# LU blocks of a mixture-of-experts stage on one core: base copied from PSUM tile to PSUM tile, ranks accumulated there, output products issued one by one

## The chip, the cores and the metric

The kernel runs on one core of one Trainium2 chip. The metric is the device time of that core in microseconds (us), as the median of several executions. One execution was also profiled; all lines below are from it. Line numbers such as L1092 are lines of the kernel before the change.

The core has five engines that run their own instruction queues in order and wait for each other by semaphores. TensorE (PE in the profile, PEld for its weight loads) multiplies matrices and writes only to PSUM. VectorE (DVE) and ScalarE (ACT) do elementwise work and read and write both SBUF and PSUM. GpSimd (POOL) does elementwise work in SBUF here and issues the gathers and scatters by index. SyncE (SP) issues the other transfers. In this kernel PSUM is cut into banks of 128 x 512 fp32 numbers. A tile of shape [128, 2, 512] takes two banks.

## The reference, cut to what matters

The input has 4 x 1024 tokens of 256 numbers. A linear-attention layer with a feed-forward part comes first, then a layer of 8 experts that share the matrices w1, w3, w2 and differ by low ranks of 16 (a1, b1, a3, b3, a2, b2):

```
x = x + layernorm(attention_and_ffn(layernorm(x)))        # 4096 tokens of 256
t = rmsnorm(layernorm(x))
probs = softmax(t @ gate_w.T); topw, topi = top_k(probs, 2); topw /= sum(topw)
base1, base3 = t @ w1.T, t @ w3.T                          # 1024 wide, shared by all experts
for each expert e:
    h1[e] = base1 + 2 * (t @ a1[e].T) @ b1[e].T
    h3[e] = base3 + 2 * (t @ a3[e].T) @ b3[e].T
    act[e] = silu(h1[e]) * h3[e]
    out[e] = act[e] @ w2.T + 2 * (act[e] @ a2[e].T) @ b2[e].T
x = x + layernorm(sum over the two chosen experts of weight[e] * out[e])
```

## The kernel before, in words

**Attention part.** The tokens are worked in 8 blocks of 512 (`BLK`). Each block passes through `front` (normalize, queries, keys), `middle` (attention, feed-forward) and, in two halves, `tail` (gate, choice of the two experts, scatter of the token rows into an array `rows` in DRAM, sorted by class).

**Expert part.** The sorted rows are taken back in 8 blocks of 512 tokens, in the order of the list `ORDER`: block 0, 1, 2 of kind LU, 3 H, 4 G, 5 H, 6 G, 7 LU. In an LU block each token has one expert among the first four and one among the last four. In the H and G blocks the two experts lie otherwise. `prepare` (L870) loads the rows of a block and builds the transposed tokens `tT`, the masks `m0` and `m1`, the weights `wt` and the ranks `u0`.

**An LU block** is worked by `experts` (L1008) in eight steps f = 0 to 7, one for each 128 of the 1024 hidden features:

1. `base(f)` (L1019) multiplies `tT` by the slices of w1 and w3 into a two-bank PSUM tile `ph`: four products of 512 columns. The tile comes from a pool with two buffers, so that step f+1 can write one while step f is read from the other.
2. `copied` (L1102) lets ScalarE copy both banks of `ph` to an SBUF tile `copy` (L1105).
3. `halved` (L1080) adds the ranks. For the expert of the lower half TensorE adds them onto `ph`. For the upper one it writes the ranks alone to a second two-bank tile `py`, and VectorE adds the copy to it (L1092, 1024 columns). Products of the lower and the upper half use 64 rows of the array each and run side by side. Then ScalarE takes tanh of the first bank of each tile (L1090, L1094), and VectorE makes the two activations in four operations (L1097, L1098).
4. `mixed` (L1071) defers three GpSimd operations (L1078) that weight the two activations into a slice of `actA` (f below 4) or `actB`.
5. `down_lu` (L1109) multiplies the activations of step f-2 by a2 into a bank `pya`, and VectorE adds that to `yacc` (L1116).

After the eight steps the stream `finishing` (L1236) takes a buffer of the pool of `ph` for the output `po` and multiplies the slices of `actA`/`actB` by w2: 32 products of 256 columns (`up`, L1163), issued in batches, and four with b2. `finish` (L1167) has ScalarE copy one half of `po` after the other to `tT` (L1177). `end` (L1183) normalizes, and GpSimd adds the residual and scatters the rows to the output (L1225, L856). The main loop of the next block starts only when all `finishing` streams are done (L1125); its first `base(0)` comes ahead of that.

**The order of the work** is written by a planner in the kernel itself when it is built. Every piece of work is a Python generator (`Stream`) that yields a time at which it may go on. `now()` counts planned TensorE time; `V`, `A` and `G` count planned time of VectorE, ScalarE and GpSimd. At each point the planner takes the first stream that may run: a side stream (`sides`, L1335: ends, preparations, tails, fronts, middles, and last `finals`, the outputs), or else the main loop of the present block. The result is one fixed order for each engine. GpSimd work is put in a list (`defer`, L218) and issued by `catch_up` (L221). While the expert blocks run, the side streams share two one-bank PSUM tiles (`ps`).

The eight PSUM banks: two one-bank tiles `ps`, two two-bank buffers for `ph` and `po`, one two-bank tile `py`.

Of the kernel before, what the change touches and what calls it, by code (L numbers as in the profile page):

```python
# [8 lines left out]
F32 = mybir.dt.float32  # L9
# [42 lines left out]
def sandwich_kernel(  # L52
# [37 lines left out]
    phh = ctx.enter_context(tc.tile_pool(name="phh", bufs=2, space=PSUM))  # L90
# [104 lines left out]
    homes = [(ps, "ps"), (ps, "ps"), (phh, "ph"), (phh, "ph"), (pyy, "py")]  # L195
# [20 lines left out]
    later = []  # L216
# [4 lines left out]
    def catch_up(key=None, soon=None):  # L221

        while later:
            if soon is not None and max(free["G"], later[0][1]) > soon:
                break
            if key is not None and key not in [k for k, *_ in later]:
                break
            _, after, cost, do = later.pop(0)
            do()
            G(cost, after)  # L230
# [60 lines left out]
    def rsqrt(mv, eps, name, after=0.0):  # L291

        n = mv.shape[1]
        a = small([P, n], "rsa", f"rsa_{name}", 8)
        r = small([P, n], "rs", f"rs_{name}", 8)
        nc.vector.tensor_scalar(a, mv[:, :, 1], eps, None, ALU.add)  # L296
        nc.gpsimd.tensor_tensor(r, a, neghalf[:, 0:n], ALU.pow)  # L297
        return a, r, G(1.1, V(0.25, after))

    def rsqrt2(mv, eps, eps2, name, tag, after=0.0):  # L300


        n = mv.shape[1]
        a = small([P, 2, n], "r2a", f"r2a_{name}", 6)
        q = small([P, n], "r2q", f"r2q_{name}", 6)
        r = small([P, 2, n], tag, f"r2_{name}", 6)
        nc.vector.tensor_scalar(a[:, 0, :], mv[:, :, 1], eps, None, ALU.add)
        nc.vector.reciprocal(q, a[:, 0, :])
        nc.vector.tensor_tensor(q, q, mv[:, :, 1], ALU.mult)
        nc.vector.tensor_scalar(a[:, 1, :], q, eps2, None, ALU.add)  # L310
        nc.gpsimd.tensor_tensor(  # L311
            r.rearrange("p a t -> p (a t)"), a.rearrange("p a t -> p (a t)"),
            neghalf[:, 0 : 2 * n], ALU.pow,
        )
        return r, G(1.1 if n < TB else 1.65, V(1.1, after))
# [402 lines left out]
    def tail(i, hf, y, mv, e):  # L718
# [105 lines left out]
        e = V(3.2)  # L824
        for j in range(HT):
            scatter(rows, to[:, j : j + 1], xt[:, o + j, :], ROWS - 1, "rows")
# [41 lines left out]
    moe, taken, ended = {}, set(), set()  # L868
# [139 lines left out]
    def experts(n, kind):  # L1008
# [10 lines left out]
        def base(f):  # L1019
            ph = phh.tile([P, 2, BLK], F32, tag="ph", name=f"ph_{n}_{f}")  # L1020
            fs = slice(f * P, (f + 1) * P)
            for a, (w, _) in enumerate(W13):
                for c in range(DC):
                    if kind == "H":

                        for h in range(2):
                            mm(ph[:, h, a * HB : (a + 1) * HB], w[:, c, fs],
                               tT[:, c, h * HB : (h + 1) * HB], a == 0 and c == 0, False,
                               skip_group_check=True)
                    else:  # L1030
                        mm(ph[:, a, :], w[:, c, fs], tT[:, c, :], c == 0,
                           kind == "LU" and c == DC - 1)
            return ph
# [37 lines left out]
        def mixed(f, acts, e):  # L1071

            ac = halves[f // 4][:, f % 4, :]
            for k, (x0, x1, op) in enumerate((
                (acts[1], acts[0], ALU.subtract), (ac, wt, ALU.mult), (ac, acts[0], ALU.add)
            )):
                defer((n, f, k), e, 1.28,
                      lambda x0=x0, x1=x1, op=op: nc.gpsimd.tensor_tensor(ac, x0, x1, op))  # L1078

        def halved(f, ph, bc):  # L1080


            fs = slice(f * P, (f + 1) * P)
            for a, (_, bw) in enumerate(W13):
                mm(ph[:, a, :], bw[low, fs], us[0][low, a, :], False, True, skip_group_check=True)
                mm(py[:, a, :], bw[high, fs], us[0][high, a, :], True, True)
            at = now() + 0.2
            catch_up((n, f - 2, 2))
            acts = [new(f"act{k}", f"act{k}_{f}") for k in range(2)]
            nc.scalar.activation(acts[0], ph[:, 0, :], AF.Tanh, scale=0.5)  # L1090
            e0 = A(0.6, at)
            nc.vector.tensor_tensor(py, py, bc, ALU.add)  # L1092
            e1 = V(1.22, at)
            nc.scalar.activation(acts[1], py[:, 0, :], AF.Tanh, scale=0.5)  # L1094
            e1 = A(0.6, e1)
            for h, act, e in ((ph, acts[0], e0), (py, acts[1], e1)):
                nc.vector.scalar_tensor_tensor(act, act, 1.0, h[:, 0, :], ALU.add, ALU.mult)  # L1097
                nc.vector.tensor_tensor(act, act, h[:, 1, :], ALU.mult)  # L1098
                e = V(1.38, e)
            return acts, e  # L1100

        def copied(f, ph):  # L1102
            bc = mp1.tile([P, 2, BLK], F32, tag="copy", name=f"copy_{n}_{f}")
            for a in range(2):
                nc.scalar.copy(bc[:, a, :], ph[:, a, :])  # L1105
                e = A(0.6, now() + 0.2 - 1.7 * (1 - a))
            return bc, e
# [11 lines left out]
        ph = base(0)  # L1119
        if kind == "LU":  # L1120
            bc, e = copied(0, ph)
        else:
            e = 0.0
        yield max(ready, e)
        yield lambda: all(f.done for f in finals)  # L1125

        py = pyy.tile([P, 2, BLK], F32, tag="py", name=f"py_{n}")
        halves = [mp1.tile([P, FC // 2, BLK], F32, tag=t, name=f"{t}_{n}") for t in ("actA", "actB")]
        pend = []
        if kind == "LU":  # L1130
            yacc = mp1.tile([P, BLK], F32, tag="yacc", name=f"yacc_{n}")
            for f in range(FC):
                if f:
                    ph = base(f)
                    bc, e = copied(f, ph)
                    yield max(e, ea - 1.0)
                if f > 1:
                    down_lu(f - 2, pend.pop(0))
                acts, ea = halved(f, ph, bc)
                mixed(f, acts, ea)  # L1140
                pend.append(acts)
                yield 0.0
            e = ea
        else:
            for f in range(FC):
                a0, e = inner(f, 0, ph)
                nxt = base(f + 1) if f < FC - 1 else None
                yield e
                a1, e = inner(f, 1, ph)
                if f:  # L1150
                    down(f - 1, pend.pop())
                pend.append((a0, a1))
                ph = nxt
                mixed(f, pend[0], e)
                yield 0.0

        o = tT.rearrange("p c n -> p (c n)").rearrange("p (t d) -> p t d", d=D)
        po = None
# [8 lines left out]
        def finish(jj, ym):  # L1167
# [15 lines left out]
        def end(jj, m):  # L1183
# [11 lines left out]
            nc.vector.tensor_scalar(a[:, 0:m], mv[:, 0:m, 1], 1e-5, None, ALU.add)  # L1195
            nc.gpsimd.tensor_tensor(r[:, 0:m], a[:, 0:m], neghalf[:, 0:m], ALU.pow)
            yield G(1.0, V(0.15))
# [36 lines left out]
        ea = e  # L1234

        def finishing():  # L1236
            nonlocal po
            po = phh.tile([P, 2, BLK], F32, tag="ph", name=f"po_{n}")
# [8 lines left out]
            if kind == "LU":  # L1247
                for f in (FC - 2, FC - 1):
                    e = down_lu(f, pend.pop(0))
                nc.vector.tensor_tensor(ym, yacc, m1, ALU.mult)  # L1250
                e = V(0.69)
            else:
                down(FC - 1, pend[0])
                y1 = new("act1", "ym1")
                if kind == "H":
                    m, w, w0 = HB, m1[:, 0:HB], m0[:, 0:HB]
                    w1_, p0, p1 = m0[:, HB:BLK], py[:, 0, 0:HB], py[:, 0, HB:BLK]
                else:
                    m, w, w0, w1_, p0, p1 = BLK, wt, m0, m1, py[:, 0, :], py[:, 1, :]
                y0, y1 = ym[:, 0:m], y1[:, 0:m]  # L1260
                nc.vector.tensor_tensor(y0, p0, w0, ALU.mult)
                nc.vector.tensor_tensor(y1, p1, w1_, ALU.mult)
                nc.vector.tensor_tensor(y1, y1, y0, ALU.subtract)
                nc.vector.tensor_tensor(y1, y1, w, ALU.mult)
                nc.vector.tensor_tensor(y0, y0, y1, ALU.add)
                e = V(3.5 * m / BLK, now() + 0.2)
# [6 lines left out]
            finish(0, ym)  # L1273
            final = n == len(ORDER) - 1
# [4 lines left out]
            finish(2, ym)  # L1279
            closing.append(Stream(always, lambda: end(2, 2) if final else end(0, TB)))  # L1280

        finals.append(Stream(always, finishing))
# [6 lines left out]
    class Stream:  # L1289
# [5 lines left out]
        def can(self):  # L1295
            if self.done or not self.may() or min(slots) > now() + 0.2:
                return False
# [16 lines left out]
    with tc.manual_schedule(engines={EN.PE, EN.DVE, EN.Activation, EN.Pool}):  # L1314
# [20 lines left out]
        def sides():  # L1335
# [7 lines left out]
            yield from finals  # L1343
# [4 lines left out]

        def wait(main=None):

            at = [s.ready for s in [*sides(), *([main] if main else [])] if not s.done]
# [4 lines left out]
        for n, (kind, _, after, _) in enumerate(ORDER):  # L1356
            while not ready[n].done:
                s = side()
# [6 lines left out]
            while not main.done:  # L1365
# [3 lines left out]
                elif main.may() and main.ready <= now():  # L1369
                    main.may = always  # L1370
                    main.step()
                else:
                    wait(main)
        while not all(f.done for f in finals):
            s = side()
# [14 lines left out]
    with tc.If(lacking > 0):  # L1390
        with tc.For_i(0, NBLK, 1) as i:
# [6 lines left out]
            for _ in experts("all", "G"):  # L1398
                pass
            for streams in (finals, closing):  # L1400
# [51 lines left out]
```

## Time and profile before

| | |
|---|---|
| median of 3 runs | 1235.14 us (1229.81 to 1235.17) |
| the profiled execution | 1235.22 us, of which 1233.3 us from the first to the last instruction |
| mean granted TensorE clock | 0.966 of full speed |
| LU blocks 0, 1, 2, from the first product into `ph` to the last | about 255 to 345, 480 to 575, 640 to 735 us |
| H, G, H, G (blocks 3 to 6) | about 735 to 1145 us |
| LU block 7 and the end | 1145 to 1233 us |
| VectorE, add of the copy (L1092) | 32 times 1229 ns |
| ScalarE, copies (L1105) | 64 times 589 ns |
| GpSimd, mixing (L1078) | 192 times 1268 to 1340 ns |

The table's times per instruction are means of the groups by line. A span of an engine in the timeline is written as start, duration, engine, line, operation and tiles; the bracket at its end gives how long the engine was idle before and what ended that. One fp32 product is executed as two passes, so four products of `base` show as x8.

### The profile page before, as it was taken

The page shows a single profiled execution, that of the slowest core. Times are in us where ns is not written, and L with a number is a line of the kernel's source. Part 1 is how long each engine was busy: PE and PEld are TensorE (multiplying, and loading weights), DVE is VectorE, ACT ScalarE, POOL GpSimd, SP SyncE. Part 2 cuts the span into 40 slices and gives each one's busy share as a digit, 9 for nine tenths or more (in the row PEclk, how much of TensorE's full clock was granted, in tenths as well). Part 3 has the DMA queues.
Part 4 walks back from the last instruction along what each step waited for, and adds up shares of the span by engine and source line. Part 5 has one row for each costly group of instructions (what it writes and reads, how often), then busy time and mean ns, then how long its engine had stood idle before and what let it go on. Part 6 is the DMA issues. An engine that isn't in the chain of part 4 may idle for free. (4 is left out here: it accounts for less than half of the span.)

```text
span 1233.3 us, 13129 instructions
## 1 busy us (share of the span) xinstructions
PE 1116.3 (91%) x4700; PEld 753.3 (61%) x4700; DVE 657.9 (53%) x1908; ACT 363.4 (29%) x696; POOL 400.4 (32%) x394
## 2 busy tenths in 40 slices
PE   6879997998998899998999889989999999999894
PEld 5658886864477676574764457756544776445333
DVE  3583676658675547657438636435342353342462
ACT  1535443423433423322233222212111121221330
POOL 2010121123431103443214433175173183452552
PEclk9999998999998999998999898999999999999998
DMA  9800001100000100100100100010010010000000
GB/s 329 182 17 18 27 23 57 53 18 27 27 1 18 53 2 17 43 10 18 53 1 26 36 8 14 14 44 1 0 35 1 1 35 1 14 22 1 18 0 19
DMA packets 25590, 39.45 MB, mean 32 GB/s; under 512 B 2352, under 2 KB 19120, under 8 KB 25520
## 3 DMA queue, kind: packets, MB, share of 16 engines
q1 hardware_dynamic: 21344, 28.88, 7.7%
q0 software_dynamic: 3072, 8.49, 1.9%
q10 hardware_dynamic: 1104, 1.19, 0.3%
q8 instruction: 39, 0.64, 0.2%
q14 instruction: 31, 0.25, 0.1%
HBM read 21.48 MB, written 17.07 MB: 31 GB/s over the span
## 5 line engine op out<-in xcount | busy, mean ns | idle before, releaser
L261 PE MATMUL ph<-tT,w_s 128*128 128x512 f32 (+1 forms) x640 | 236.3, 517 | 6.9 <-DVE act L1040 4.4
L261 PEld LDWEIGHTS ph<-tT,w_s 128*128 128x128 f32 x640 | 120.2, 193 | 106.7 <-issue 93.6
L261 PE MATMUL ph<-u,b_s 64*128 64x256 f32 (+2 forms) x512 | 165.7, 518 | 17.1 <-DVE act L1040 8.9
L261 PEld LDWEIGHTS ph<-u,b_s 64*128 64x128 f32 (+1 forms) x512 | 69.2, 192 | 99.0 <-issue 62.8
L261 PE MATMUL pf<-h2T,wff_s 128*128 128x256 f32 x512 | 117.9, 385 | 6.5 <-DVE u L981 4.1
L1039 DVE SCALAR_TENSOR_TENSOR act<-act,ph 128x512 f32<-128x512 f32 x64 | 44.0, 688 | 147.6 <-ACT act L1037 147.6
L261 PE MATMUL py<-wff2d,g 128*128 128x256 f32 x512 | 115.7, 379 | 0.0
L261 PEld LDWEIGHTS pf<-h2T,wff_s 128*128 128x128 f32 x512 | 96.7, 191 | 24.8 <-issue 8.6
L261 PEld LDWEIGHTS py<-wff2d,g 128*128 128x128 f32 x512 | 97.4, 190 | 13.1
L1037 ACT ACTIVATE act<-ph 128x512 f32<-128x512 f32 x64 | 38.2, 597 | 162.5 <-PE ph L261 143.7
L856 POOL DMA_INDIRECT rows<-x,to x32 | 33.0, 1030 | 158.5 <-DVE to L823 53.8
L311 POOL TENSOR_TENSOR r_x<-r2a_x,neghalf 128x4 f32<-128x4 f32 (+1 forms) x24 | 30.8, 1285 | 150.7 <-DVE r2a_x L310 124.7
L675 ACT ACTIVATE g<-pf,bff 128x256 f32<-128x256 f32 x128 | 53.1, 471 | 87.1 <-PE pf L261 87.0
L1078 POOL TENSOR_TENSOR actB<-act,act 128x512 f32<-128x512 f32 x32 | 41.7, 1304 | 102.4 <-DVE act L1040 61.3
L261 PE MATMUL po<-w_s,actA 128*128 128x256 f32 x256 | 65.1, 399 | 6.5 <-ACT tT L1177 6.5
L297 POOL TENSOR_TENSOR rs_y<-rsa_y,neghalf 128x2 f32<-128x2 f32 x16 | 12.8, 798 | 176.3 <-DVE rsa_y L296 153.5
L261 PE MATMUL po<-w_s,actB 128*128 128x256 f32 x256 | 63.5, 387 | 5.7 <-POOL actB L1078 5.7
L261 PE MATMUL py<-u,b_s 64*128 64x512 f32 x128 | 67.1, 647 | 0.0
L261 PEld LDWEIGHTS po<-w_s,actA 128*128 128x128 f32 x256 | 49.2, 198 | 23.3 <-ACT tT L1177 9.7
L701 DVE SCALAR_TENSOR_TENSOR x<-py,std,x 128x256 f32<-128x256 f32 x32 | 15.4, 483 | 89.2 <-PE py L261 89.2
L1092 DVE TENSOR_TENSOR py<-py,copy 128x1024 f32<-128x1024 f32 x32 | 39.3, 1229 | 37.0 <-PE py L261 37.0
L261 PEld LDWEIGHTS po<-w_s,actB 128*128 128x128 f32 x256 | 49.4, 194 | 14.7 <-POOL actB L1078 6.7
(256 smaller groups left out, 1900.4 us busy)
## 6 DMA issues: line engine op xcount, KB each, us to landing
rows<-none SPq DMA_DIRECT2D x1, 4192.0 KB, 24.1
kept<-x SPq DMA_DIRECT2D x16, 262.0 KB, 2.1
row<-rows SPq DMA_DIRECT2D x8, 524.0 KB, 4.2
z<-in_x_dram SPq DMA_DIRECT2D x8, 512.0 KB, 3.4
x<-in_x_dram SPq DMA_DIRECT2D x8, 512.0 KB, 4.7
w_s<-in_w_dram SPq DMA_DIRECT2D x3, 1024.0 KB, 12.3
wff_s<-in_wff_dram SPq DMA_DIRECT2D x2, 1024.0 KB, 10.7
b_s<-in_b_dram SPq DMA_DIRECT2D x2, 512.0 KB, 11.5
```

The lines of the kernel that those rows point to most:

```text
L261: nc.tensor.matmul(out_, lhsT=lhsT, rhs=rhs, start=start, stop=stop, **kw)
L297: nc.gpsimd.tensor_tensor(r, a, neghalf[:, 0:n], ALU.pow)
L311: nc.gpsimd.tensor_tensor(r.rearrange("p a t -> p (a t)"), a.rearrange("p a t -> p (a t)"), neghalf[:, 0 : 2 * n], ALU.pow,)
L675: nc.scalar.activation(g[:, k * W : (k + 1) * W], pf[:, k * W : (k + 1) * W], AF.Gelu_apprx_tanh, bias=bff1_s[:, f : f + 1],)
L701: nc.vector.scalar_tensor_tensor(y[:, j, :], py[:, D : 2 * D], std[:, j : j + 1], y[:, j, :], ALU.mult, ALU.add)
L856: ins = nc.gpsimd.indirect_dma_start(out=dst[:, :], out_offset=bass.IndirectOffsetOnAxis(ap=at, axis=0), in_=src, in_offset=None, bounds_c ...
L1037: nc.scalar.activation(th, h1, AF.Tanh, scale=0.5)
L1039: nc.vector.scalar_tensor_tensor(th, th, 1.0, h1, ALU.add, ALU.mult)
L1078: lambda x0=x0, x1=x1, op=op: nc.gpsimd.tensor_tensor(ac, x0, x1, op))
L1092: nc.vector.tensor_tensor(py, py, bc, ALU.add)
```

## The change

It does five things.

- **The base goes from `ph` to `py` by ScalarE, and TensorE adds both ranks.** `base(f, ph, a)` now makes one half (a = 0: w1, a = 1: w3). After each half ScalarE copies that bank of `ph` to the same bank of `py`. The upper ranks are accumulated onto `py` as the lower ones onto `ph`. The VectorE addition (L1092) and the SBUF copy go away. In step 0 of block 0 the base of `py` is instead computed a second time by TensorE.
- **Two single buffers in place of a pool of two.** The tags `ph0` and `ph1` have one buffer each. An LU block uses one of them (`mine`) for all of its `ph`, and the other is for the output `po`.
- **Output products as a stream.** `output` yields after every single product, and the planner takes it (`filler`) only when neither a side stream nor the main loop can run. An LU block starts once the block before it has released `py` (`left`), with that block's outputs still to come.
- **GpSimd's list** is issued ahead of a power operation or a scatter where it is planned to be through by then (`catch_up(by=e)`).
- **Last block, step 7:** the three mixing operations run on VectorE. `down_lu` takes step f-1 in place of f-2.

```
-    phh = ctx.enter_context(tc.tile_pool(name="phh", bufs=2, space=PSUM))
+    phh = ctx.enter_context(tc.tile_pool(name="phh", bufs=1, space=PSUM))
...
-    def catch_up(key=None, soon=None):
+    def catch_up(key=None, soon=None, by=None):
...
+            if by is not None and max(free["G"], now(), later[0][1]) + later[0][2] > by + 0.3:
+                break
...
-        def halved(f, ph, bc):
+        def halved(f, ph):
             fs = slice(f * P, (f + 1) * P)
             for a, (_, bw) in enumerate(W13):
-                mm(ph[:, a, :], bw[low, fs], us[0][low, a, :], False, True, skip_group_check=True)
-                mm(py[:, a, :], bw[high, fs], us[0][high, a, :], True, True)
+                for bank, r in ((ph, low), (py, high)):
+                    mm(bank[:, a, :], bw[r, fs], us[0][r, a, :], False, True, skip_group_check=True)
...
-            nc.vector.tensor_tensor(py, py, bc, ALU.add)
...
+            for f in range(FC):
+                if f % 4 == 0:
+                    yield lambda: n == 0 or upped.get(n - 1, 0) >= f + 4
+                    value_tiles(f // 4)
+                yield e
+                ph = banks(mine, f"ph_{n}_{f}")
+                for a in range(2):
+                    base(f, ph, a)
+                    if n + f:
+                        nc.scalar.copy(py[:, a, :], ph[:, a, :])
+                        e = A(0.6, max(e1, now() + 0.2))
+                    else:
+                        base(f, py, a)
+                yield e - 0.4
+                if f:
+                    down_lu(f - 1, pend)
+                pend, (e, e1) = halved(f, ph)
+                mixed(f, pend, e1)
+                yield 0.0
...
+        def output(ahead):
+            nonlocal po
+            yield lambda: ahead is None or ahead.done
+            po = banks(1 - mine, f"po_{n}")
+            for f in range(FC):
+                yield lambda: (n, f, 2) in at_end
+                yield at_end[n, f, 2]
+                for j in range(TB):
+                    up(j, f)
+                    if j == TB - 1:
+                        upped[n] = f + 1
+                    yield 0.0
...
+                elif main.can(False):
                     main.step()
+                elif filler():
+                    filler().step()
```

H and G blocks keep their loops and their batched output (now named `rest`). They take the buffers of `ph` in turn (`whole_base`, `pair`), and the first `base` of a G block now stands ahead of the output products of the H block before it.

## The prediction

> **What bounds the kernel now.** I read the busy shares first, then TensorE's waits, then the timeline of the last LU block, where nothing but the block itself runs.
>
> ```profile
> span 1233.3 us, 13129 instructions
> PE 1116.3 (91%) x4700; PEld 753.3 (61%) x4700; DVE 657.9 (53%) x1908; ACT 363.4 (29%) x696; POOL 400.4 (32%) x394
> ```
>
> TensorE is busy for 91%, and the change takes no product away. It can only remove TensorE's idle time (117 us) or add to it. So I count the waits of TensorE, before and after.
>
> ```profile
> PE ph L261 <- ACT copy L1105: 8.2, 11, 2.6
> ...
> PE po L261 <- POOL actB L1078: 5.7, 2, 3.0
> ```
>
> (Total us, times, longest us.) The wait for the copy that the change works on is small: 8.2 us. Now one step of the last block:
>
> ```profile
> 1170.13 0.69 PE L261 MATMUL ph<-u,b_s 64*128 64x512 f32 x1 [0.21 <-ACT copy L1105]
> ...
> 1172.05 3.70 PE L261 MATMUL ph<-tT,w_s 128*128 128x512 f32 x8
> 1172.21 0.60 ACT L1090 ACTIVATE act<-ph 128x512 f32<-128x512 f32 x1 [2.13 <-PE py L261]
> 1172.26 1.23 DVE L1092 TENSOR_TENSOR py<-py,copy 128x1024 f32<-128x1024 f32 x1 [1.60 <-PE py L261]
> ...
> 1175.44 0.69 DVE L1098 TENSOR_TENSOR act<-act,py 128x512 f32<-128x512 f32 x1
> ...
> 1175.68 1.08 PE L261 MATMUL pya<-act,a_s 128*64 128x512 f32 x4
> 1175.84 1.07 ACT L1105 COPY copy<-ph 128x512 f32<-128x512 f32 x2 [1.72 <-PE ph L261]
> ...
> 1176.97 0.69 PE L261 MATMUL ph<-u,b_s 64*128 64x512 f32 x1 [0.21 <-ACT copy L1105]
> ```
>
> The next base (1172.05) runs while ScalarE and VectorE still work on this step, until 1176.13: two buffers allow it. The beat is 1176.97 - 1170.13 = 6.84 us, nearly all of it products. The third thing to see is what TensorE does between two banks of one tile:
>
> ```profile
> 1211.92 1.03 PE L261 MATMUL po<-b_s,ym 128*128 128x256 f32 x4
> 1212.99 0.60 ACT L1177 ACTIVATE tT<-po 128x512 f32<-128x512 f32 x1 [11.52 <-PE po L261]
> ...
> 1213.64 1.99 PE L261 MATMUL po<-w_s,actA 128*128 128x256 f32 x8 [0.69 <-ACT tT L1177]
> ```
>
> ScalarE reads the first bank of `po`, and TensorE, whose next products go to the second bank, waits for it to end. Issue of the four passes ends at 1211.92 + 4 x 0.213 = 1212.77 (a 512-column pass takes 0.427, by the eight passes from 1172.05 on), so this costs 0.87 us.
>
> **The change, part by part.**
>
> *The copy between the two base halves.* In the instruction order of the changed kernel as built, the first w3 product of `base` waits for ScalarE's copy of the w1 half, in all 31 steps that copy. It is the situation of the last fence: same tile, other bank. Nothing can fill it, since no other product stands between. Price: 0.87 each (0.24 until ScalarE starts, 0.59 the copy, 0.05 back). No row shows ScalarE writing PSUM. The nearest rows are this copy as the second of a pair, 0.53, and tanh, 0.60, so 0.81 to 0.88. I take 0.87. Blocks 0 to 2 have 23: +20.0. Block 7 is counted by its beat.
>
> On this the Trainium skill speaks ("PSUM — Partial Sum Buffer", summary): guard PSUM by bank, and read a bank other than the one a matmul writes. By that page the w3 half could run during the copy and the sum would be 27 us lower. The 0.69 row shows that programs of this kind wait although the bank differs.
>
> *One `ph` instead of two.* `base` of step f+1 must now wait until VectorE has read `ph` of step f. With R the start of a step's rank products: ScalarE starts at R + 2.08 (1172.21 - 1170.13), tanh takes 0.60, and two VectorE operations of 0.69 with some 0.05 before each free `ph` at R + 4.15. The rank products end at R + 1.7, so about 2.3 us of other products have to lie there. I counted them in the built order. In blocks 0 to 2 attention work fills every such place but one (block 2, step 2 to 3, with nothing): +2.3. After the second base half, the 1.08 us of `pya` cover the copy's 0.88.
>
> *The beat of block 7.* Base starts at R + 4.2; w1 half 0.11 + 1.71, wait 0.89, w3 half 1.71 (to R + 8.6), `pya` 1.08: next R after 9.75 us. Where the order puts two output products (0.85) in front of `pya`, 10.6. Places as built: 9.75 three times, 10.6 three times, once 10.2 (one product). Sum 71.3, against 1197.48 - 1145.57 = 51.9 from the first to the last step before. +19.4, and 0.9 for the wait of step 0: +20.3.
>
> *The end.* Before, 35.8 us pass from the last step's rank products (1197.48) to the end of the span. After: activations done at R + 5.5 (two more operations on VectorE), three mixing operations on VectorE at 0.69 instead of GpSimd's 1.27 (R + 7.6), the last four output products (behind those of step 6) to R + 10.0, two of b2 to R + 10.9, ScalarE to R + 11.7, two more of b2 behind the same kind of wait to R + 12.6, second read-out at 12.85. From there to the end it was 1233.3 - 1218.26 = 15.0. So 27.9: -7.9.
>
> *Base of `py` by TensorE in step 0 of block 0:* four products more, 8 x 0.427 = +3.4. The built order has 2598 products against 2594.
>
> *What goes away.* The waits for the old copy in blocks 0 to 2, two of them, 1.2 and 1.4: -2.65. The 5.7 us in which output products waited for GpSimd around 580 us: a stream that is taken only when its operands are planned ready shouldn't stand there; I take all of it, with nothing as the other end. VectorE's 32 x 1.23 = 39 us (L1092) cost nothing now, since TensorE's idle time isn't VectorE's there; they shorten its queue. Other waits of TensorE (over 0.4 us) inside the three blocks' stretches sum to 18.8 us. The 23 new stops let the other engines catch up, and VectorE is freer: between 0 and 18.8 of them go; I take 3, since most of these waits end a chain that starts with a product (product, read-out, next product) and so moves along with TensorE. GpSimd's new order, and H and G, whose outputs only change places with a `base`: 0, hidden under products that stay as they are.
>
> **Sum:** 20.0 + 2.3 + 20.3 - 7.9 + 3.4 - 2.65 - 5.7 - 3.0 = +26.8. On 1233.3 that is a span of 1260; 1.9 us lie around it in this execution, whose 1235.22 is the median's 1235.14. Forecast **1262 us**.
>
> **A second effect, the clock.**
>
> ```profile
> 1161.65 0.69 PE L261 MATMUL ph<-u,b_s 64*128 64x512 f32 x1 [2.61 <-ACT copy L1105]
> ...
> 1164.06 4.86 PE L261 MATMUL ph<-tT,w_s 128*128 128x512 f32 x8
> ```
>
> After 2.61 us of idle, eight passes took 4.86 instead of 3.70; with the late start the step lost 1.6 us. Gaps of 2.2 us (at 944 and 1120 us) had no such sequel. Block 7 gets three gaps of 2.4 us: between 0 and +5; I take 0 and put 5 into the range. The Trainium skill ("TensorE: Matmul & The Clock Gate", Part 1) halves the clock after an idle window of about 3.4 us and so would charge nothing here; the 2.61 row already differs.
>
> **Rivals.**
>
> *The new stops displace the old ones (about 1245).* All 18.8 go instead of 3: 1262 - 16 = 1246; with the cheaper copy (0.81) in 31 steps 1244, and with a quarter of the 19.5 us of such waits that lie between the blocks 1239. For it: TensorE runs less far ahead. Against: VectorE's queue in block 0 is full (side work between every two steps), whoever waits.
>
> *VectorE late for the single buffer (about 1282).* If one side operation of 0.7 us (L636) stands ahead of the two that free `ph`, each of 23 steps loses 0.7: +16, and +5 by the clock: 1283. For it: the full queue just named. Against: the planner places base only when it thinks `ph` free, and runs ahead of real time by the stops it doesn't know.
>
> *Faster (about 1229): the output stream fills the holes.* Blocks 0 to 2 have 96 single products of 0.43, 41 us that can go into any hole. Between 240 and 840 us TensorE's waits over 0.4 sum to 44. If all go: 20.0 + 2.3 + 20.3 - 7.9 + 3.4 - 44 = -6. It decides from 38 of the 44. Against: side work was there to fill these holes before, too; they are waits that the planner didn't foresee, and a stream chosen by the same plan sees them no better.
>
> **How the numbers follow.** Forecast 0.54 (1250 to 1274), displaced 0.22, VectorE late 0.18, faster 0.06. Of the displaced case 0.08 lies within 0.5% (6 us, about what a measurement of this kernel can tell from no change). Faster 0.06, same 0.08, slower 0.86. The range takes in most of the displaced case, down to 1242, and the late one at 1283.
>
> **What would show it.** In the changed profile, w3 products of `ph` should show an idle time of some 0.7 us before them, ended by ScalarE's copy, 31 times; block 7 should beat at 9.7 to 10.6 us; the end should shorten by 8. If the second base half starts with no gap, or the beat stays below 9, the forecast is too high. If TensorE's other waits between 240 and 740 us fall by 15 or more, the first rival holds; if `ph` waits for VectorE (L1105 of the changed kernel) in blocks 0 to 2, the second.

## The result, and the profile after

The changed kernel takes 1269.2 us (median of 4, 1267.87 to 1271.76), the kernel before, measured with it, 1235.16. The ratio is 1.0288, 95% interval 1.0255 to 1.0321. The page of the changed kernel begins:

```profile
span 1267.9 us, 13070 instructions
...
PE 1126.7 (89%) x4708; PEld 747.6 (59%) x4708; DVE 654.9 (52%) x1879; ACT 362.4 (29%) x694; POOL 399.7 (32%) x391
```

The span grew by 34.6 us. TensorE is busy for 10.4 us more (eight passes more, and slower ones behind some gaps, see the last section) and idle for 24.2 more. What it waits for has a new first line (us in total, times, longest us):

```profile
PE ph L263 <- ACT py L1299: 46.0, 31, 6.8
PE ph L263 <- DVE act L1105: 12.6, 8, 2.2
```

31 waits for the bank-to-bank copy are the 31 steps that copy. But they sum to 46.0 us, 1.48 each, where one such wait in the last block is 0.66. GpSimd's `actB` (5.7 us before) is gone from the list.

Next, the same three stretches of both kernels: blocks 0 to 2 (from the first product into `ph` to the first rank product of block 3), the H and G blocks, block 7 to the end. The columns are the stretch, its length, the busy time and count of PE, PEld, DVE, ACT and POOL, the granted clock, the DMA share and GB/s. The kernel before:

```profile
258.37:787.06 528.69, 480.74 (x2025) 325.16 (x2023) 319.09 (x1015) 168.79 (x334) 160.26 (x142) 0.96 0.06 22
787.06:1145.57 358.51, 339.97 (x1367) 207.41 (x1366) 139.94 (x266) 68.69 (x121) 158.71 (x135) 0.99 0.04 14
1145.57:1233.30 87.73, 67.09 (x225) 31.21 (x224) 42.78 (x71) 21.89 (x39) 43.61 (x39) 0.91 0.04 13
```

The changed one:

```profile
259.04:808.71 549.67, 482.32 (x2029) 320.25 (x2027) 319.48 (x987) 167.22 (x330) 162.97 (x142) 0.97 0.06 21
808.71:1167.28 358.57, 343.44 (x1371) 207.57 (x1370) 143.02 (x271) 69.64 (x122) 158.96 (x135) 0.98 0.04 14
1167.28:1267.90 100.62, 70.85 (x225) 30.35 (x224) 36.88 (x66) 21.64 (x39) 39.84 (x36) 0.93 0.03 11
```

Blocks 0 to 2 take 21.0 us longer, the H and G blocks the same, block 7 12.9 longer. One step of block 7 in the timeline of the changed kernel:

```profile
1177.02 0.69 PE L263 MATMUL ph<-u,b_s 64*128 64x512 f32 x1
...
1179.04 0.60 ACT L1101 ACTIVATE act<-ph 128x512 f32<-128x512 f32 x1 [0.31 <-PE py L263]
...
1181.13 1.98 PE L263 MATMUL ph<-tT,w_s 128*128 128x512 f32 x4 [1.06 <-DVE act L1105]
...
1183.15 0.57 ACT L1299 COPY py<-ph 128x512 f32<-128x512 f32 x1 [3.03 <-PE ph L263]
...
1183.77 1.98 PE L263 MATMUL ph<-tT,w_s 128*128 128x512 f32 x4 [0.66 <-ACT py L1299]
...
1185.59 1.03 PE L263 MATMUL po<-w_s,actA 128*128 128x256 f32 x4
...
1187.56 0.69 PE L263 MATMUL ph<-u,b_s 64*128 64x512 f32 x1
```

With R the start of the step's rank products, the base starts at R + 4.1, when VectorE has read the single `ph`. The w3 half waits for the copy of the w1 half, and the next ranks come 10.54 us after the last.

The excess over 0.66 lies in blocks 0 to 2. The longest of the 31 waits, in the timeline of the changed kernel:

```profile
589.11 1.88 PE L263 MATMUL ph<-tT,w_s 128*128 128x512 f32 x4
...
595.85 0.19 DVE L326 SCALAR_TENSOR_TENSOR lm_x<-mv_x,rs_x 128x4 f32<-128x4 f32 x1
...
596.17 1.09 ACT L341 ACTIVATE x<-x,lm_x,rs_x 128x256 f32<-128x256 f32 x2 [10.96 <-DVE lm_x L326]
...
597.16 0.57 ACT L1299 COPY py<-ph 128x512 f32<-128x512 f32 x1
...
597.79 3.66 PE L263 MATMUL ph<-tT,w_s 128*128 128x512 f32 x4 [6.80 <-ACT py L1299]
```

The w1 half is done at 590.99, and ScalarE has been idle for 10.96 us, but its queue is in order: two normalizes stand ahead of the copy, and they wait for statistics that VectorE has late. So TensorE waits 6.80 us for a copy of 0.57. Then its four passes take 3.66 instead of 1.98.

### The profile page after: what moved, and what is told of

It reads as the page before. It is cut to its first block, busy times and chain, and to the rows that moved or that the text cites. A ratio compares the mean times of both kernels' runs of the same rounds, so it can differ in the third digit from the quotient of the medians.

```text
span 1267.9 us, 13070 instructions
## 1 busy us (share of the span) xinstructions
PE 1126.7 (89%) x4708; PEld 747.6 (59%) x4708; DVE 654.9 (52%) x1879; ACT 362.4 (29%) x694; POOL 399.7 (32%) x391
## 4 chain that ended last, share of the span: by engine, by line
PE 74%; DVE 15%; ACT 6%; issue 2%; POOL 1%; DMA 1%; another core or an unknown queue 0%; SPq 0%; POOLq 0%; DVEq 0%; ACTq 0%
PE ph L263 26%; PE py L263 14%; PE po L263 8%; PE pf L263 8%; PE pz L263 3%; PE pya L263 2%; DVE act L1105 2%; PE pu L263 2%; PE pk L263 2%; DVE act L1104 2%; PE pq L263 2%; PE pa L263 1%; ACT py L1299 1%; ACT act L1101 1%; PE pt_h L276 1%
## 5 line engine op out<-in xcount | busy, mean ns | idle before, releaser
L263 PE MATMUL ph<-tT,w_s 128*128 128x512 f32 (+1 forms) x640 | 252.0, 534 | 63.4 <-ACT py L1299 46.0
L263 PEld LDWEIGHTS pf<-h2T,wff_s 128*128 128x128 f32 x512 | 96.0, 190 | 20.5 <-issue 5.6
L1089 POOL TENSOR_TENSOR actA<-act,act 128x512 f32<-128x512 f32 x32 | 41.8, 1306 | 173.0 <-DVE act L1105 71.0
L317 POOL TENSOR_TENSOR r_x<-r2a_x,neghalf 128x4 f32<-128x4 f32 (+1 forms) x24 | 30.8, 1285 | 139.0 <-DVE r2a_x L314 112.5
L1299 ACT COPY py<-ph 128x512 f32<-128x512 f32 x62 | 35.4, 572 | 127.9 <-PE ph L263 127.9
## 6 DMA issues: line engine op xcount, KB each, us to landing
rows<-none SPq DMA_DIRECT2D x1, 4192.0 KB, 23.2
b_s<-in_b_dram SPq DMA_DIRECT2D x2, 512.0 KB, 11.6
```

Of the source, the lines that this page charges most:

```text
L263: nc.tensor.matmul(out_, lhsT=lhsT, rhs=rhs, start=start, stop=stop, **kw)
L317: nc.gpsimd.tensor_tensor(r.rearrange("p a t -> p (a t)"), a.rearrange("p a t -> p (a t)"), neghalf[:, 0 : 2 * n], ALU.pow,)
L1299: nc.scalar.copy(py[:, a, :], ph[:, a, :])
```

## The experiments

Theory: the stop between the base halves sets the loss in blocks 0 to 2, and its price is the copy plus whatever stands in ScalarE's queue. The main rival: it only took the place of other waits. All stages in one table (us of the profiled execution; the side work can cross the border at block 3, so the first two stretches are added; ratios are to the kernel before as measured with each run, 1233.94 to 1235.87, with 95% intervals):

| kernel | median | ratio | first `ph` to block 7 | block 7 to the end |
|---|---|---|---|---|
| before | 1235.16 | | 887.2 | 87.7 |
| changed | 1269.2 | 1.0288 (1.0255 to 1.0321) | 908.2 | 100.6 |
| e1, both halves first | 1225.94 | 0.9945 (0.9922 to 0.9969) | 869.0 | 96.9 |
| e2, copy alone | 1232.22 | 0.9993 (0.9969 to 1.0017) | 889.8 | 84.0 |
| e3, SBUF copy back | 1254.78 | 1.0163 (1.0119 to 1.0207) | 892.9 | 105.0 |
| e6, copy twice | 1293.35 | 1.0475 (1.0431 to 1.0519) | 925.6 | 108.5 |
| e4, tiles by half | 1213.68 | 0.9826 (0.9787 to 0.9865) | 860.5 | 90.5 |
| e7, GpSimd's order back | 1225.49 | 0.9915 (0.9880 to 0.9949) | 868.8 | 98.5 |
| e8, outputs batched | 1294.79 | 1.0488 (1.0448 to 1.0528) | 920.2 | 111.6 |
| e9, two buffers in block 7 | 1213.98 | 0.9836 (0.9794 to 0.9879) | 864.1 | 86.0 |
| e10, normalizes off ScalarE | 1243.98 | 1.0086 (1.0052 to 1.0119) | 876.3 | 101.0 |
| e11, e4 and e9 together | 1208.98 | 0.9799 (0.9766 to 0.9831) | 862.9 | 86.0 |

The two stage columns come from one execution each. e1 and e9 issue the same products in the same order up to block 7 and still differ by 4.9 us there, so differences of that size in the first of them say little by themselves.

### e1: both halves first, then both copies

```
                 for a in range(2):
                     base(f, ph, a)
                     if n + f:
-                        nc.scalar.copy(py[:, a, :], ph[:, a, :])
                         e = A(0.6, max(e1, now() + 0.2))
                     else:
                         base(f, py, a)
+                if n + f:
+                    for a in range(2):
+                        nc.scalar.copy(py[:, a, :], ph[:, a, :])
```

> Both base halves are issued first and then both bank-to-bank copies; everything else as in the changed kernel, so its single ph and its output stream stay. Theory (the wait between the halves costs 31 fixed stops): no w3 product of ph waits for ScalarE's copy any more; blocks 0 to 2 lose 23 x 0.87 = 20 us, block 7 some 5 us (a beat of 9.2 instead of 9.74, 9.7 instead of 10.6, since pya then covers most of the two copies): about 1244 us, and 1239 if the 5 us of late copies in ScalarE's queue go too. If the copies are only covered by pya (1.08 us against 1.43), 23 x 0.35 = 8 us come back as waits before the rank products: 1252. Rival (the stops only took the place of other waits, which come back): 1260 or more, with TensorE's other waits in blocks 0 to 2 up by 15 us or more.

1225.94 us: 43 us less than the changed kernel, and 0.55% less than the kernel before. The order of TensorE's products is that of the changed kernel. The stretches of this run:

```profile
258.66:769.90 511.24, 475.12 (x2029) 320.68 (x2028) 319.72 (x987) 167.80 (x330) 162.42 (x142) 0.98 0.07 23
769.90:1127.66 357.76, 340.24 (x1372) 206.24 (x1371) 143.00 (x271) 69.59 (x122) 158.74 (x135) 0.99 0.04 14
1127.66:1224.60 96.94, 70.91 (x225) 31.59 (x224) 36.84 (x66) 21.60 (x39) 39.83 (x36) 0.91 0.03 12
```

Its waits hold only this of the copy, before the rank products:

```profile
PE ph L263 <- ACT py L1305: 0.8, 3, 0.3
```

In blocks 0 to 2 the stop cost 38.4 us (549.7 against 511.2), nearly twice the 20 of the forecast. TensorE is 7.2 us less busy there (482.3 against 475.1) and 31.2 less idle. The idle time does not fall by all the 40.8 us of copy waits in this stretch: summed over the timeline, the other waits are 26.3 us with the stop and 35.7 without it. So 9.4 us of other waits had been displaced. The rival is right to that extent and no more. Block 7 gained 3.7, with beats of 9.13 to 9.71 where the clock held, as expected.

### e6: the copy of the w1 half twice

```
-                        nc.scalar.copy(py[:, a, :], ph[:, a, :])
+                        for _ in range(2 - a):
+                            nc.scalar.copy(py[:, a, :], ph[:, a, :])
```

> The changed kernel with the copy of the w1 half issued twice (the result is the same): 31 more copies of 0.57 us, all in the stop between the halves. Theory (unfillable stop): each step longer by 0.57 us, 31 x 0.57 = +17.7 us, 1287 us, 13 of it in blocks 0 to 2 and 4 in block 7. Rival (the stops are absorbed by slack elsewhere in blocks 0 to 2): +9 us or less, 1278 or less, with block 7 alone showing its 4.

1293.35 us, 24 more than the changed kernel. The waits answer to the dose almost exactly:

```profile
PE ph L263 <- ACT py L1300: 63.3, 31, 7.4
```

+17.3 against 31 x 0.57 = 17.7: nothing fills the stop. The expected time was 6 us too low; TensorE is busy for 7.2 us more (1133.9 against 1126.7) on the same products. The mean granted clock is 0.961 against 0.969, as more groups run slow (last section).

### e10: the normalizes taken out of ScalarE's queue

```
             else:
-                nc.scalar.activation(
-                    dst[:, j, :], src[:, j, 0:D], AF.Identity, bias=lm[:, k : k + 1],
-                    scale=r[:, k : k + 1],
-                )
+                nc.vector.tensor_scalar(
+                    dst[:, j, :], src[:, j, 0:D], r[:, k : k + 1], lm[:, k : k + 1],
+                    ALU.mult, ALU.add,
+                )
                 ends.append(A(0.6, lm_end))
```

The same is done in `normed` and `end`.

> The changed kernel, stop between the halves included, in the same order of issue; only the 134 normalizes of 0.59 us that stand in ScalarE's queue (x, z, y, the expert inputs and the outputs) are done by VectorE instead. Read is the wait of the w3 half, not the time, since VectorE gets some 50 us more to do. Theory (eight of the 31 waits were long, 26 us over the usual 0.66, because the copy stood in ScalarE's queue behind normalizes that waited for VectorE's statistics): the 31 waits sum to 22 to 28 us instead of 46.0, and the four longest (3.98, 6.80, 4.19, 5.32) are gone, below 2. Rival (the long waits have another cause, such as the copy waiting for py to be free): the sum stays at 40 or more.

The wait, and the place that had cost 6.80 us:

```profile
PE ph L263 <- ACT py L1299: 23.2, 31, 1.9
```

```profile
583.94 0.57 ACT L1299 COPY py<-ph 128x512 f32<-128x512 f32 x1 [5.76 <-PE ph L263]
...
584.57 1.98 PE L263 MATMUL ph<-tT,w_s 128*128 128x512 f32 x4 [0.66 <-ACT py L1299]
```

23.2 us instead of 46.0. The one long wait that stays (1.94, at 337.74) follows two ScalarE operations of the queries, which were not moved. So the excess over 31 x 0.66 = 20.5 was ScalarE's queue: of 25.5 us, 22.8 went with the normalizes. The time fell by 25 us although VectorE got 50 us more to do (705.2 against 654.9).

### e4: one tile for each half

```
+                tiles = (banks(mine, f"ph_{n}_{f}"),
+                         pyy.tile([P, 2, BLK], F32, tag="py", name=f"py_{n}_{f}"))
...
+                            mm(tiles[a][:, k, :], w[:, c, fs], tT[:, c, :], c == 0, c == DC - 1)
                     if n + f:
-                        nc.scalar.copy(py[:, a, :], ph[:, a, :])
+                        nc.scalar.copy(tiles[a][:, 1, :], tiles[a][:, 0, :])
```

The tile still tagged `ph` holds both banks of the w1 half, `py` both of w3. VectorE does its two additions of 1 first, so that `ph` is free as early as before.

> The changed kernel in its own order (copy between the base halves), but with the four banks paired the other way: one tile holds the two banks of the w1 half, the other tile the two of the w3 half, so that the w3 products write another tile than the one that is being copied. Theory (the stop comes from both halves lying in one tile, for which the built program sets a wait, and not from the chip): the w3 products follow at once, block 7 beats at 8.8 us (9.7 where two output products stand before pya), blocks 0 to 2 are as with both halves first: 1222 us (1217 to 1228). Rival (TensorE and ScalarE can't use neighbouring banks at one time): the w3 half starts late or takes longer than 1.7 us, or the copy longer than 0.57, in all 31 steps, and the time stays above 1240.

1213.68 us, below the expected 1217 to 1228. A step of block 7 in its timeline:

```profile
1163.78 1.98 PE L263 MATMUL ph<-tT,w_s 128*128 128x512 f32 x4 [1.78 <-DVE act L1104]
...
1165.60 1.88 PE L263 MATMUL py<-tT,w_s 128*128 128x512 f32 x4
...
1165.80 0.57 ACT L1304 COPY ph<-ph 128x512 f32<-128x512 f32 x1 [3.46 <-PE ph L263]
...
1167.32 1.03 PE L263 MATMUL po<-w_s,actA 128*128 128x256 f32 x4
```

The w3 half follows with no idle time and takes 1.88; the copy runs beside it and takes 0.57 as ever. So TensorE can write one bank while ScalarE copies between two others, and the stop is a wait that the program sets because both banks belong to one tile. (Which banks are neighbours is not on record, so this isn't shown for every pair.) What the prediction cited from the Trainium skill ("PSUM — Partial Sum Buffer", summary) fits this run as a statement on the chip. It does not describe the program built from the change. In block 7 the gain on e1 is a beat of 8.40 to 9.27 (once 10.34, a step with two groups of output products) and a gap before the base of 1.78 instead of 2.19, after which no group ran slow. The shorter gap comes with the new pairing too: tanh needs only the ranks of the `ph` tile, which stand first (1.2 us after their start instead of 2.0), and VectorE reads that tile first. Of the 8.5 us up to block 7 some is the clock (three slow groups behind gaps in e1, one here), and against e9, which has e1's order up to there, only 3.6 are left. The medians of e1 and e4 are 12.3 us apart and block 7 has 6.4 of it, which leaves some 6 for the rest; where they lie is not shown.

### e2: the bank-to-bank copy alone in the kernel before

```
-            nc.vector.tensor_tensor(py, py, bc, ALU.add)
...
-                nc.scalar.copy(bc[:, a, :], ph[:, a, :])
+                nc.scalar.copy(py[:, a, :], ph[:, a, :])
```

The upper ranks are accumulated on `py` as in the change; two buffers, batched outputs and the old loop stay. In step 0 of block 0 TensorE computes the base of `py`, as in the change.

> The kernel before with one part of the change alone: base copied bank to bank after both halves, ranks added by TensorE on py, VectorE's addition gone; two ph buffers, batched output products and the old loop stay. Theory (the part is harmless where it makes no stop between the halves): block 7 keeps its beat of 6.8 us, the base of py by TensorE costs 3.4 us, the shorter queue of VectorE gives back between 0 and 18: 1222 to 1240, likeliest 1229. Rival (the bank-to-bank copy itself, or the rank products that wait for it, are what is dear): the beat of block 7 rises to 8 us or more, and the time to 1250 or more.

1232.22 us, no difference that can be measured. Block 7 beats at 6.88. With two buffers VectorE's addition lay beside other work, and taking away its 39 us, for four products more on TensorE, gives no gain that shows.

### e3: the addition back in the changed kernel

```
-                        nc.scalar.copy(py[:, a, :], ph[:, a, :])
+                    nc.scalar.copy(bc[:, a, :], ph[:, a, :])
...
+            nc.vector.tensor_tensor(py, py, bc, ALU.add)
```

> The changed kernel with the copy to SBUF and VectorE's addition of 1.23 us back, both halves of the base issued together; the single ph, the output stream and VectorE's last mixing stay. Theory (the stop between the halves costs 20 us in blocks 0 to 2, the single ph costs block 7 its beat): no wait between the halves, block 7 still at 9.4 to 10.3 us a step, blocks 0 to 2 shorter by about 20, and 3.4 us less for the base of py: 1243. The addition comes back into the chain that frees the single ph, so up to 23 x 0.6 = 14 us may come back as waits of ph for VectorE: 1257 at most. Rival (the stops displaced other waits): 1260 or more. If the single ph and the stream were harmless, block 7 would be back at 7 us a step and the time at or below 1235.

1254.78 us, near the upper end of what was expected. It differs from e1 in the addition and the place of the copy, and in the four products of step 0 that it doesn't need (both issue both halves first). It is 29 us slower; in the profiled execution, the slowest of its four, 24 up to block 7 and 8 in it. So the same addition that e2 found to be free is dear in the changed kernel. How it costs that is shown only in part. In block 7 the waits of `ph` for VectorE grow from 9.1 to 11.6 us. In blocks 0 to 2, which take 30.8 us longer (the H and G blocks 6.9 less), they stay at 3.7 against 3.6: there the products take 14.1 us longer, and the rest is waits spread over many tiles of the side work.

### e7 and e8: which part gained

e7 takes the `catch_up(by=e)` calls out of e1. e8 batches its output products:

```
+            yield lambda: (n, FC - 1, 2) in at_end
+            yield at_end[n, FC - 1, 2]
             for f in range(FC):
-                yield lambda: (n, f, 2) in at_end
-                yield at_end[n, f, 2]
                 for j in range(TB):
                     up(j, f)
-                    if j == TB - 1:
-                        upped[n] = f + 1
-                    yield 0.0
+            upped[n] = FC
```

> Both base halves first, and GpSimd's order as it was before the change (mixing is not drawn ahead of the powers and scatters). With both halves first the kernel took 1225.9. Theory A (what the change gained in blocks 0 to 2 comes from the output products going out one by one): about the same, 1221 to 1231. Theory B (it comes from GpSimd's order): the 18 us of those blocks come back, 1240 or more.

> Both base halves first, and the 32 output products of an LU block issued in one batch once the last values are mixed, as before the change. With both halves first and single products: 1225.9. Theory A (the single output products made the gain in blocks 0 to 2): blocks 0 to 4 and the rest up to block 7 lose the 18 to 21 us that they had gained, and block 7 some 5 us (its end is 10 us longer, its beats 9.1 us throughout): 1250 (1243 to 1256). Theory C (the gain is that of the shorter VectorE queue or of the single ph): only block 7 changes, 1231.

e7 took 1225.49: GpSimd's order makes no difference that shows. e8 took 1294.79, 69 us more than e1, where 24 were expected. The direction is theory A's, the size is not. TensorE's waits for the single `ph` double:

```profile
PE ph L263 <- DVE act L1105: 25.3, 15, 2.2
```

and the mean granted clock falls to 0.952 (0.975 in e1): the same products take 27.1 us longer (1142.7 against 1115.6). The rest is idle time. As batching costs 51 us up to block 7, where e1 had gained 18 on the kernel before, it does more than undo the single products; what part of it is the blocks' later starts was not tried.

### e9 and e11: block 7 with two buffers

e9 is e1 with this for the last block only; its output products follow the last base, and its `down_lu` takes step f-2 again:

```
-                ph = banks(mine, f"ph_{n}_{f}")
+                ph = banks((mine + f) % 2 if final else mine, f"ph_{n}_{f}")
```

> Both base halves first; in block 7 alone the steps alternate between the two pairs of banks, as before the change, and its output products follow the last base. Theory (the single ph costs block 7 about 2.3 us a step, the output products in its holes give back 7 at the end): beat 6.9 instead of 9.1 to 9.7, end 35 instead of 27.8, block 7 from 96.9 to 83; 1211 us (1206 to 1217), faster than both kernels. Rival (block 7 is bound by its products in sum, so that what the beat gains the end loses): 1222 or more.

1213.98 us. Block 7 beats at 6.88 (8.70 and 7.03 once each) and ends 35.9 us after its last ranks, as before the change: 86.0 us against 96.9. e11 joins it with e4 for the other blocks.

> Both cures together: in blocks 0 to 2 one tile for each half, the copy beside the w3 half; in block 7 two pairs of banks in turn, with both halves first and the output products after the last base. Theory (the two act in different stages and add): 505.0 + 355.5 for the stages before block 7 as in the run with tiles by half, 86.0 - 1.7 for block 7 as in the run with two buffers less the one slow step there: 1208 us (1204 to 1213). Rival (block 7 takes back what the blocks before gained, since their side work then falls into it): 1213 or more.

1208.98 us, as expected: 2.0% faster than the kernel before and 4.7% faster than the changed one (1208.98 / 1269.2). It is the best version found. That the total fits so well is partly luck: its stages are 4 us longer than the expected sum (862.9 + 86.0 against 860.5 + 84.3), and what stands before the first `ph`, the same work in both, was 4.7 us shorter than in e4. By the medians it is 5 us below e9 alone, by the traces only 1.2 up to block 7, so it is not shown where joining the two gains.

## Why the prediction came out as it did

The total was near (1262 against 1269.2), but that is partly luck: two of its terms were wrong in opposite directions. By its own steps:

- **The copy between the halves, 0.87 x 31 and unfillable.** The wait was there 31 times and unfillable, as e6 shows. The 0.87 holds where ScalarE is free: the profile counts 0.66 as idle, from the modelled end of the last pass, and the beat of block 7 came out as the 0.87 had made it. The step that failed is the sentence that priced all 31 alike: "0.24 until ScalarE starts" takes ScalarE's queue to be empty each time, read from the last block, where it is. In blocks 0 to 2 the stops cost 38.4 us instead of 20.0 (e1): copies stood behind other ScalarE work, eight of them for long, 25.5 us in all, and 22.8 of these were normalizes (e10). So the copy waits sum to 40.8 us there; 9.4 us of other waits were displaced by them, and 7.2 us of slower products come on top.
- **What goes away, 2.65 + 5.7 + 3.** Under-sized too: the other waits of blocks 0 to 2 fell from 47.8 us to 26.3, by 21.5. 9.4 of these were displaced by the stop (e1 has them back); 12 are a lasting gain, and TensorE's products take 5.6 us less in e1 (475.1 against 480.7) although four were added. Without the stop blocks 0 to 2 take 17.5 us less than in the kernel before (511.2 against 528.7), where the forecast's other terms make 5.65 less (2.3 + 3.4 - 2.65 - 5.7 - 3). So the stop was 18.4 us too low and the relief 11.9 too low. The difference, some 6.6, is all that shows in blocks 0 to 2: +21.0 against a forecast of +14.35. Two executions can differ by 5 us here, so the two errors are sure and their exact sizes are not. That the lasting gain comes from the single output products is argued from e8 and from e7, which rules out GpSimd's order; the products as a stream beside two buffers of `ph` were not run.
- **One `ph`: one empty place, +2.3.** Two waits of this kind in blocks 0 to 2, 1.49 us at 273.2 and 2.12 at 705.0. Nearly right while the stream fills the places: in e8 there are eight, 10.1 us.
- **The beat of block 7.** 9.74, 10.54, 10.60, 10.17 against 9.75, 10.6, 10.2. One of the seven steps took 12.27, by the clock. Sum 72.8 against 71.3.
- **The end.** 27.8 us from the last ranks against 27.9.
- **H and G, GpSimd's order: 0.** 358.6 against 358.5; e7 confirms the second.
- **VectorE's addition at nothing.** Right for two buffers (e2), which is the kernel that the prediction said it of. In the changed kernel it is worth 29 us (e3 against e1).
- **The clock.** The prediction took 0 and said that gaps of 2.2 us at 944 and 1120 us had no sequel. At 944 that was a misreading of the kernel before: the four passes there took 3.67 us instead of 1.98.

```profile
944.55 3.67 PE L261 MATMUL ph<-u,b_s 128*128 128x512 f32 x4 [2.19 <-DVE act L1040]
```

The rivals: "displaced" holds for 9.4 us. Its sign, other waits between 240 and 740 us down by 15 or more, did appear (44.9 to 25.2), but the sign can't tell waits that the stop displaced from waits that are gone for good; e1 can. "VectorE late" shows in the two waits of `ph` above, 3.6 us instead of 16. The "faster" case failed because of the stop; its mechanism was real in part, with 12 us of waits gone for good of the 44 that it counted on. Against it stood that a stream chosen by the same plan would see unforeseen waits no better, and that argument falls in part: with the stop gone the same stream and single `ph` are 20.8 us shorter up to block 7 than e2, and batching takes that away.

## What to carry to other kernels

A short operation put between two products costs the whole time until its engine gets to it, here up to 6.80 us for a copy of 0.57: count what stands ahead of it in that engine's queue and what those wait for, however low the engine's busy share is. Two banks in one tile are one thing to the program that sets the waits; put what must run side by side into different tiles. Price the parts of a change together, since here an addition was free in the old kernel and dear in the changed one. A single buffer cost 3.6 us in three blocks with side work to fill its waits, and some 11 in the one block without any (e9 against e1).

## What the runs showed of the hardware

The clock fell after shorter gaps than I had expected, and not always. In the 12 profiles of this case I took each group of three or more passes of 128 rows by 512 columns behind an idle time of TensorE of 1.4 us or more. After 1.4 to 2.0 us none of 24 groups ran slow (over 1.2 times the usual time). After 2.1 to 2.25 us 37 of 57 did, and after 2.5 us or more 13 of 15. Two gaps of one size in the changed kernel, each with its four passes in the timeline and the busy times of the same stretch, whose third number from the end is the granted clock, 1.00 and 0.54:

```profile
1171.45 1.98 PE L263 MATMUL ph<-tT,w_s 128*128 128x512 f32 x4 [2.19 <-DVE act L1105]
```

```profile
1171.45:1173.43 1.98, 1.98 (x4) 0.68 (x4) 1.91 (x5) 0.00 (x0) 0.57 (x1) 1.00 0.00 0
```

```profile
1191.73 3.65 PE L263 MATMUL ph<-tT,w_s 128*128 128x512 f32 x4 [2.18 <-DVE act L1105]
```

```profile
1191.73:1195.38 3.65, 3.65 (x4) 1.17 (x4) 1.23 (x2) 0.00 (x0) 3.33 (x4) 0.54 0.20 72
```

A fully slow group costs about 1.7 us. e1 and e9 issue the same products up to there, and the gap of 2.18 us near 1101 us was followed by four passes of 3.66 us in e1 and of 1.98 in e9. The Trainium skill ("TensorE: Matmul & The Clock Gate", Part 1) puts the idle window at about 3.4 us and describes it as free-running, which would fit a sequel that comes and goes. Its length does not fit these rows, in which gaps of 2.2 us were followed by products at about half speed.
